# Exponentials written into the tile that will hold the state, four states ahead, and scanned in place

## The chip, the core and the metric

The kernel runs on one core of one Trainium2 chip. The metric is the device time of one execution in microseconds (us). Before the change three timed runs took 11246.39, 11232.78 and 11244.71 us; the median is 11244.71 us. The core has five engines that each work through their own list of instructions in order and wait for one another by semaphores: TensorE (PE in the profile, its weight loads PEld), VectorE (DVE), ScalarE (ACT), GpSimd (POOL), and SyncE (SP), which issues the DMAs.

## The reference, cut to what matters

The program is a two-layer block on eight images of 64x64 pixels with 96 channels. What fills the time is the selective scan of the first layer, which runs along four orders of the pixels (`K` = 4: two diagonals, each in both directions), over 192 channels with 16 states for each channel:

```python
delta = jax.nn.softplus(dts + dt_projs_bias[None, :, :, None])
A = -jnp.exp(A_logs).reshape(K, D_INNER, D_STATE)
...
def step(hst, inp):
    u_t, d_t, B_t, C_t = inp
    hst = hst * jnp.exp(d_t[..., None] * A) + (d_t * u_t)[..., None] * B_t[:, :, None, :]
    return (hst, jnp.einsum('bkdn,bkn->bkd', hst, C_t))
```

For every channel and every state n this is a first-order recurrence along the 4096 pixels: the decay `exp(delta * A_n)` multiplies the old state, the feed `delta * u * B_n` is added, and the result times `C_n` is summed over the 16 states. Around it lie a group norm, a projection, a 3x3 convolution, a layer norm and an output projection; after it come linear attention and a feed-forward layer.

## The kernel before, in words

**Steps and states.** One image is cut into 8 chunks of 512 pixels, and each chunk is scanned once forwards (q = 0) and once backwards (q = 1). That makes 8 x 2 x 8 = 128 steps. A step has 16 states (n = 0 to 15, here called places), so the main loop of `run` (line 1155) passes 2048 states, numbered i = 16m + n. A tile of one state is 128 partitions by 3 groups by 512 pixels: two diagonals with 64 channels each on the partitions, 192 = 3 x 64 channels in the groups g = 0, 1, 2.

**What one state needs.**
- `decay(i)` (line 961): three exponentials on ACT, one for each group, line 966.
- The feed, which stands in three PSUM banks, `feed[0]` to `feed[2]`, that all states share. It is made in one of three ways, by the letter of the place in `FEED = "DADADAGADADAAAAA"` (line 48). Letter A (10 places): eight copies with a scale on ACT, line 988, write the tile feedT (two buffers), and `turn(i, g)` transposes it into bank g, four transposes for each group, line 996. Letter G (place 6): the same with three products on POOL (line 979). Letter D (places 0, 2, 4, 8 and 10): ACT makes nothing; one matmul (line 998) spreads a row into `feed[0]`, and three products on DVE (line 1013) fill the three banks.
- `recur(i)` (line 1000): three scans on DVE (line 1009), one for each group; each reads its decays, its feed bank and the last column of the step before (carry), and writes the state tile h.
- `keep(i)` and `read(i)` (lines 1021 and 1027): POOL copies the last column into carry (line 1025) and multiplies h in place by the row C (line 1030; the row comes by two DMAs of `fetch`, line 952).
- `reduce(i, part)` (line 1032): PE transposes h and sums it in PSUM, twelve transposes in three parts of four, line 1044. Every part reads columns of all of h, so h is free only after part 2.

**The order.** Nothing is reordered by a scheduler: each engine executes in the order in which the loop writes the instructions. Iteration i of the loop writes
- for ACT: `decay(i+2)`, then other stages' ACT work (`work.at("A")`), then the eight copies of `times_b(i+2)`;
- for DVE: the products and scans of state i, with other stages' DVE work ahead of the third scan;
- for PE: `turn(i+1, 0)`, `reduce(i-4, 0)`, other work, `turn(i+1, 1)`, `reduce(i-4, 1)`, other work, `turn(i+1, 2)`, `reduce(i-4, 2)`, other work;
- for POOL: `keep(i-1)` and `read(i-1)`; for SP: `fetch(i+4)`.

The other work comes from `Work` (line 261), which hands out pieces of the remaining stages of the neighbouring images by a credit in microseconds for each iteration: the convolution (line 542), the walk along the diagonals (lines 587 to 596), the tail (lines 608 to 836), and `prologue` (line 879), which makes rows, delta and du of a step that is about two steps ahead. The longest pieces on ACT are softplus (line 921, with a load of a table before and after it) and SiLU (lines 558 and 559).

**Buffers around the change.** Tiles come from a pool; a tile's tag has a fixed number of buffers, used in turn, and the first instruction that writes a new tile waits until the last instruction that uses the buffer's old tile has ended. Before, decays have three buffers and h has six. So `decay(i+2)` takes the buffer of `decay(i-1)` and waits for the third scan of state i-1, and the first scan of state i takes the buffer of h(i-6). In all 3 + 6 = 9 tiles of 128 x 1536 float32.

Of the kernel before, what the change touches and what calls it, by code (L numbers as in the profile page):

```python
# [9 lines left out]
F32 = mybir.dt.float32  # L10
F16 = mybir.dt.float16
F8 = mybir.dt.float8e5
AF = mybir.ActivationFunctionType
ALU = mybir.AluOpType
# [3 lines left out]
P = 128  # L18
# [13 lines left out]
T = 512  # L32
# [3 lines left out]
G = 3  # L36
# [802 lines left out]
def run(tc, psum, dram, x, out, w, NB):  # L839
# [9 lines left out]
    nc = tc.nc  # L849
    scans = ExitStack()  # L850
    pool = scans.enter_context(tc.tile_pool(name="scan", bufs=1))
# [3 lines left out]
    total = len(steps) * NS  # L855
# [15 lines left out]
            )  # L871
        return images[b]

    made, decays, feeds, hs, carry, sums, other = {}, {}, {}, {}, {}, {}, {}
    feed = [psum.tile([P, T], F32, tag=f"feed{g}", name=f"feed{g}") for g in range(G)]
    banks = [psum.tile([P, T], F32, tag=f"bank{i}", name=f"bank{i}") for i in range(2)]
    work = Work(banks + feed)
# [62 lines left out]
    def bring(m):  # L940

        b, q, c = steps[m]
        work.finish(lambda: c in image(b).walked)
        u = pool.tile([P, G, T], F32, tag="u", name=f"u_{m}", bufs=2)
        made[m] = SimpleNamespace(u=u, c={}, multiplied=False)
        for d in range(2):
            nc.sync.dma_start(
                out=u[d * GC : (d + 1) * GC],
                in_=image(b).seq[d][:, c * T : (c + 1) * T].rearrange("(g i) t -> i g t", i=GC),
            )  # L950

    def fetch(i):

        m, n = divmod(i, NS)
        cc = made[m].c[n] = pool.tile([P, T], F32, tag="cc", name=f"cc_{i}", bufs=5)
        for d in range(2):
            nc.sync.dma_start(
                out=cc[d * GC : (d + 1) * GC], in_=made[m].crow[d * NS + n : d * NS + n + 1, :].to_broadcast([GC, T])
            )

    def decay(i):
        m, n = divmod(i, NS)
        _, q, _ = steps[m]
        decays[i] = pool.tile([P, G, T], F32, tag="decay", name=f"decay_{i}", bufs=3)
        for g in range(G):
            nc.scalar.activation(decays[i][:, g, :], made[m].delta[:, g, :], AF.Exp, scale=w.a_neg[:, q, g, n : n + 1])  # L966

    def times_b(i):

        m, n = divmod(i, NS)  # L970
        o = made[m]
        if FEED[n] == "D":
            return
        f = feeds[i] = pool.tile([P, TB * G, P], F32, tag="feedT", name=f"feedT_{i}", bufs=2)
        if FEED[n] == "G":
            d = 2
            scale = o.rows[:, :, XB : XB + d * NS].rearrange("p j (d n) -> p j d n", d=d)[:, :, :, n]
            for g in range(G):
                nc.gpsimd.tensor_tensor(  # L979
                    f.rearrange("p (j g) (d c) -> p g j d c", g=G, d=d)[:, g],  # L980
                    o.duT.rearrange("p (j g) (d c) -> p g j d c", g=G, d=d)[:, g],
                    scale.unsqueeze(3).to_broadcast([P, TB, d, GC]), ALU.mult,
                )
            return
        for j in range(TB):
            for d in range(2):
                part = (slice(None), slice(j * G, (j + 1) * G), slice(d * GC, (d + 1) * GC))
                nc.scalar.activation(  # L988
                    f[part], o.duT[part], AF.Copy, scale=o.rows[:, j, XB + d * NS + n : XB + d * NS + n + 1]
                )  # L990

    def turn(i, g):
        m, n = divmod(i, NS)
        if FEED[n] != "D":
            for j in range(TB):
                nc.tensor.transpose(feed[g][:, j * P : (j + 1) * P], feeds[i][:, j * G + g, :], w.ident)  # L996
        elif g == 0:
            nc.tensor.matmul(feed[0], w.pick[:, FEED[:n].count("D"), :], made[m].x, start=True, stop=True)  # L998

    def recur(i):  # L1000
        m, n = divmod(i, NS)
        _, q, _ = steps[m]
        h = hs[i] = pool.tile([P, G, T], F32, tag="h", name=f"h_{i}", bufs=6)
        a = decays.pop(i)
        back = slice(None, None, -1) if q else slice(None)

        def scan(g):
            init = carry[m - 1][:, n, g : g + 1] if m % NST else 0.0
            nc.vector.tensor_tensor_scan(h[:, g, back], a[:, g, back], feed[g][:, back], init, ALU.mult, ALU.add)  # L1009

        if FEED[n] == "D":
            for g in (1, 2, 0):
                nc.vector.tensor_tensor(feed[g], feed[0], made[m].du[:, g, :], ALU.mult)  # L1013
        if n == FEED.rindex("D"):
            made[m].multiplied = True
        scan(0)
        scan(1)
        work.at("V")
        scan(2)
# [12 lines left out]
    def reduce(i, part):  # L1032
        m, n = divmod(i, NS)
        b, q, c = steps[m]
        if n == 0 and part == 0:
            sums[m] = psum.tile([P, TB * G, P], F32, tag="y", name=f"y_{m}")
        if q and n == 8 and part == 0:
            other[m] = pool.tile([P, TB * 2 * DI], F32, tag="y0", name=f"y0_{m}")
            nc.sync.dma_start(out=other[m], in_=image(b).part[:, c, :])
        y = sums[m]  # L1040
        some = range(4 * part, 4 * part + 4)
        for j in some:
            r, g = divmod(j, G)
            nc.tensor.matmul(  # L1044
                y[:, j, :], hs[i][:, g, r * P : (r + 1) * P], w.ident, is_transpose=True,
                start=(n == 0 and j % 4 == 0), stop=(n == NS - 1), skip_group_check=True,
            )
        if q and n in (1, 2, 3) and part == 2:
            for j in range(4 * (n - 1), 4 * n):
                r, g = divmod(j, G)  # L1050
                nc.tensor.matmul(
                    y[:, j, :], made[m].u[:, g, r * P : (r + 1) * P], w.skip[:, g, :],
                    start=False, stop=False, skip_group_check=True,
                )
        if part == 2:
            hs.pop(i)

    def place(m):

        b, q, c = steps[m]
        y = sums.pop(m)
        ys = pool.tile([P, TB * 2 * DI], F32, tag="ys", name=f"ys_{m}")
        rows = ys.rearrange("p (d k c) -> p d k c", d=2, k=TB)
        for d in range(2):
            nc.scalar.copy(
                rows[:, d].rearrange("p k (g i) -> p k g i", i=GC),
                y.rearrange("p (k g) (d i) -> p d k g i", g=G, d=2)[:, d],
            )  # L1070
        if q == 0:
            nc.sync.dma_start(out=image(b).part[:, c, :], in_=ys)
        else:
            work.start(spread(m, rows), urgent=True)
# [20 lines left out]
    def before(b):  # L1095
        return measures(tc, work, pool, x, w, image(b), b)
# [4 lines left out]
    def between(b):  # L1101
        if b + 1 < NB:
            yield from begin(b + 1)
        if b > 0:
            yield from end(b - 1)
# [17 lines left out]
    def all_done():  # L1123
        return not (work.streams or work.jobs)
# [20 lines left out]
    LAG = 4  # L1145
    for i in range(4):
        fetch(i)
    for i in range(2):
        decay(i)
        times_b(i)  # L1150
    for g in range(G):
        turn(0, g)
# [2 lines left out]
    for i in range(total + LAG + 1):  # L1155
        m, n = divmod(i, NS)
        b, at = divmod(i, PER)
        if i < total:
            if at == LAG + 3 and b:
                work.finish(lambda: all_done() and not other)  # L1160
                work.finish(all_done)
                work.stream(between(b))
            if at == PER // 2 and b + 2 < NB:
                work.stream(before(b + 2))
            if n == NS - 3 and m + 2 < len(steps):
                work.start(prologue(m + 2), urgent=True)
            if n == NS // 2 and m + 2 < len(steps):
                bring(m + 2)
        work.next()
        if i + 2 < total:  # L1170
            decay(i + 2)
        work.at("A")
        if i + 2 < total:
            times_b(i + 2)
        if i < total:
            recur(i)
        else:
            work.at("V")
        for part in range(3):
            if i + 1 < total:  # L1180
                turn(i + 1, part)
            if 0 <= i - LAG < total:
                reduce(i - LAG, part)
            work.at("P", part)
        if 0 <= i - LAG < total and (i - LAG) % NS == NS - 1:
            place((i - LAG) // NS)
        if 0 <= i - 1 < total:
            keep(i - 1)
            read(i - 1)
        work.at("G")  # L1190
        if i + 4 < total:
            fetch(i + 4)
        feeds.pop(i, None)
# [86 lines left out]
```

## Time and profile before

| what | value |
|---|---|
| median of three timed runs | 11244.71 us |
| profiled execution, span from first to last instruction | 11243.9 us |
| mean granted TensorE clock in it | 0.907 of full speed |
| start of the first scan, end of the last scan | 244.2 us, 10996.3 us |
| scans (line 1009) | 6144, 1201 to 1262 ns each |
| exponentials (line 966) | 6144, 714 ns each |
| copies of feedT (line 988) | 10240, 445 ns each |
| transposes of feedT and of h (lines 996 and 1044) | 16896 and 24576 |
| products of h with C on POOL (line 1030) | 2048, 3457 ns each |

The page gives the span of the profiled execution; its own time as a whole is not listed apart, and the span is 0.8 us below the median of the timed runs. Of the span, 10752 us lie between the first and the last scan: 5.25 us for one state, 84.0 us for one step. The table of waits lists for each pair "engine, tile and line of who waited <- who ended the wait" the total in us, how often, and the longest. In a timeline each line has the start and the duration in us, the engine, the line of the kernel, the operation, the tile written and the tiles read, the shapes and the count of merged instructions; in square brackets stands how long the engine had been idle just before, and what ended that.

### The profile page before, as it was taken

To read this page: it belongs to the slowest core of one execution; us is meant where nothing else is said; L and a number is where in the kernel's file an instruction comes from. 1 tells how busy PE (TensorE), PEld (TensorE's weight loads), DVE (VectorE), ACT (ScalarE), POOL (GpSimd) and SP (SyncE) were. 2 spreads that over 40 slices of the span, in tenths; PEclk is the share of its full clock that TensorE was granted. 3 is DMA by queue.
4 is the path that set the end of the run, shared out by engine and by line. 5 is a ranking of instruction groups with operands and counts; after the bars stand their busy time and mean duration, and the time that the engine had idled before them with its cause. 6 is when DMAs were issued, how large, how long until landed. Compare 5 with 4: busy or idle time off the path is not lost.

```text
span 11243.9 us, 182845 instructions
## 1 busy us (share of the span) xinstructions
PE 9140.0 (81%) x60885; PEld 7661.4 (68%) x60885; DVE 9396.9 (84%) x10582; ACT 9455.9 (84%) x19651; POOL 9365.4 (83%) x7047
## 2 busy tenths in 40 slices
PE   6888788878888788878888788887888878878884
PEld 5677677666676667766677666776667666666663
DVE  2988988888888888888888888888898888989993
ACT  3888888888888888888888888888898888888883
POOL 1877987899878998789987899779997799998994
PEclk8999999888998889988999898998999988889886
DMA  3335333543335443354334543345433543432332
GB/s 91 106 92 143 100 98 92 144 118 102 97 93 149 110 108 95 96 144 113 102 92 113 138 107 102 92 118 134 109 99 90 133 119 104 108 103 84 99 94 63
DMA packets 1122742, 1206.98 MB, mean 107 GB/s; under 512 B 452790, under 2 KB 730007, under 8 KB 1121799
## 3 DMA queue, kind: packets, MB, share of 16 engines
q1 hardware_dynamic: 1121798, 1195.28, 40.3%
q8 instruction: 485, 7.95, 0.3%
q14 instruction: 459, 3.75, 0.1%
HBM read 874.83 MB, written 319.98 MB: 106 GB/s over the span
## 4 chain that ended last, share of the span: by engine, by line
PE 24%; ACT 23%; DVE 17%; POOL 14%; issue 10%; DMA 7%; SPq 4%; DVEq 0%; POOLq 0%; ACTq 0%
DVE h L1009 11%; ACT feedT L988 9%; POOL h L1030 8%; ACT decay L966 7%; PE y L1044 7%; PE feed L996 7%; DMA cc<-crow 4%; DVE feed L1013 4%; PE bank L542 3%; SPq L587 2%; PE bank L894 2%; PE feed L998 1%; ACT L63 1%; POOL du L928 1%; DMA y<-wide 1%
## 5 line engine op out<-in xcount | busy, mean ns | idle before, releaser
L1030 POOL TENSOR_TENSOR h<-h,cc 128x1536 f32<-128x1536 f32 x2048 | 7079.9, 3457 | 458.3 <-DMA cc<-crow 228.9
L1009 DVE TENSOR_TENSOR_SCAN h<-decay,carry,feed 128x512 f32<-128x512 f32 x5376 | 6514.2, 1262 | 810.2 <-PE feed L996 704.8
L966 ACT ACTIVATE decay<-delta,a_neg 128x512 f32<-128x512 f32 x6144 | 3975.0, 714 | 1116.4 <-DVE h L1009 1114.4
L996 PE MATMUL feed<-ident,feedT 128*128 128x128 f32 x16896 | 3090.8, 303 | 1649.1 <-DVE h L1009 1084.6
L1044 PE MATMUL y<-ident,h 128*128 128x128 f32 x24576 | 3847.4, 290 | 130.7 <-POOL h L1030 47.4
L996 PEld LDWEIGHTS feed<-ident,feedT 128*128 128x128 f32 x16896 | 2209.1, 155 | 2246.9 <-ACT feedT L988 840.8
L988 ACT ACTIVATE feedT<-duT,rows 128x192 f32<-128x192 f32 x10240 | 3673.7, 445 | 17.6 <-PE feed L996 14.7
L1044 PEld LDWEIGHTS y<-ident,h 128*128 128x128 f32 x24576 | 3164.5, 152 | 525.2 <-issue 410.3
L1013 DVE TENSOR_TENSOR feed<-feed,du 128x512 f32<-128x512 f32 x1920 | 1200.4, 685 | 162.2 <-PE feed L998 146.5
L1025 POOL COPY carry<-h 128x3 f32<-128x3 f32 x2048 | 402.5, 197 | 877.0 <-DVE h L1009 803.2
L1009 DVE TENSOR_TENSOR_SCAN h<-decay,feed 128x512 f32<-128x512 f32 x768 | 879.5, 1201 | 118.9 <-PE feed L996 106.8
L542 PE MATMUL bank<-wf,xp 97*128 97x192 f32 x4266 | 851.9, 332 | 0.0
L998 PE MATMUL feed<-x,pick 77*128 77x512 f32 x1280 | 708.8, 636 | 3.9
L542 PEld LDWEIGHTS bank<-wf,xp 97*128 97x128 f32 x4266 | 692.8, 194 | 5.4 <-issue 4.6
L928 POOL TENSOR_TENSOR du<-delta,u 128x1536 f32<-128x1536 f32 x128 | 448.4, 3503 | 188.8 <-ACT delta L921 188.8
L916 PE MATMUL bank<-x,ws 13*128 13x512 f32 x764 | 435.5, 650 | 5.6 <-ACT x L907 5.6
L979 POOL TENSOR_TENSOR feedT<-duT,rows 128x512 f32<-128x512 f32 x384 | 396.2, 1060 | 4.7 <-PE feed L996 4.7
L894 PE MATMUL bank<-wx,u 128*128 128x77 f32 x3048 | 360.0, 275 | 0.0
L894 PEld LDWEIGHTS bank<-wx,u 128*128 128x128 f32 x3048 | 352.3, 193 | 1.9 <-ACT duT L936 0.2
L918 DVE COPY delta<-bank 128x512 f32<-128x512 f32 x382 | 256.7, 672 | 86.5 <-PE bank L916 86.1
L934 PE MATMUL bank<-ident,du 128*128 128x128 f32 x1532 | 251.8, 291 | 65.1 <-POOL du L928 61.8
L998 PEld LDWEIGHTS feed<-x,pick 77*128 77x128 f32 x1280 | 211.5, 200 | 97.6 <-DVE h L1009 44.8
(261 smaller groups left out, 6957.4 us busy)
## 6 DMA issues: line engine op xcount, KB each, us to landing
cc<-crow SPq DMA_DIRECT2D x4096, 128.0 KB
u<-seq SPq DMA_DIRECT2D x256, 384.0 KB
wide<-ys SPq DMA_DIRECT2D x512, 192.0 KB
ut<-image SPq DMA_DIRECT2D x768, 64.0 KB
seq<-us SPq DMA_DIRECT2D x128, 384.0 KB
part<-ys SPq DMA_DIRECT2D x64, 768.0 KB
y<-part SPq DMA_DIRECT2D x64, 768.0 KB
y<-wide SPq DMA_DIRECT2D x256, 192.0 KB
```

Of the source, the lines that this page charges most:

```text
L542: nc.tensor.matmul(v[:, j, :], flat[:, o : o + P], k.wf[:, i, :], start=(i == 0), stop=(i == 8), skip_group_check=True)
L894: nc.tensor.matmul(v[:, j, :], u[:, g, j * P : (j + 1) * P], w.wx[:, q, g, :], start=(g == 0), stop=(g == G - 1))
L916: nc.tensor.matmul(ps, w.ws[:, q, g, :], x[0 : 2 * NR + 1, :], start=True, stop=True)
L928: nc.gpsimd.tensor_tensor(du, delta, u, ALU.mult)
L966: nc.scalar.activation(decays[i][:, g, :], made[m].delta[:, g, :], AF.Exp, scale=w.a_neg[:, q, g, n : n + 1])
L988: nc.scalar.activation(f[part], o.duT[part], AF.Copy, scale=o.rows[:, j, XB + d * NS + n : XB + d * NS + n + 1])
L996: nc.tensor.transpose(feed[g][:, j * P : (j + 1) * P], feeds[i][:, j * G + g, :], w.ident)
L998: nc.tensor.matmul(feed[0], w.pick[:, FEED[:n].count("D"), :], made[m].x, start=True, stop=True)
L1009: nc.vector.tensor_tensor_scan(h[:, g, back], a[:, g, back], feed[g][:, back], init, ALU.mult, ALU.add)
L1013: nc.vector.tensor_tensor(feed[g], feed[0], made[m].du[:, g, :], ALU.mult)
L1030: nc.gpsimd.tensor_tensor(hs[i], hs[i], c.unsqueeze(1).to_broadcast([P, G, T]), ALU.mult)
L1044: nc.tensor.matmul(y[:, j, :], hs[i][:, g, r * P : (r + 1) * P], w.ident, is_transpose=True, start=(n == 0 and j % 4 == 0), stop=(n == NS ...
```

## The change

The tag decay with its three buffers is gone, and h has nine buffers. `decay(i)` takes the h tile and writes the exponentials into it; the scan reads its decays from h and writes the states over them. In the loop `decay(i+4)` stands where `decay(i+2)` stood, and four states' decays are written ahead of the loop where it was two. `times_b(i+2)`, the turns, the reductions and everything else keep their places. The buffer of `decay(i+4)` is now that of state i-5.

```diff
     def decay(i):
         m, n = divmod(i, NS)
         _, q, _ = steps[m]
-        decays[i] = pool.tile([P, G, T], F32, tag="decay", name=f"decay_{i}", bufs=3)
+        h = hs[i] = pool.tile([P, G, T], F32, tag="h", name=f"h_{i}", bufs=9)
         for g in range(G):
-            nc.scalar.activation(decays[i][:, g, :], made[m].delta[:, g, :], AF.Exp, scale=w.a_neg[:, q, g, n : n + 1])
+            nc.scalar.activation(h[:, g, :], made[m].delta[:, g, :], AF.Exp, scale=w.a_neg[:, q, g, n : n + 1])
...
     def recur(i):
         m, n = divmod(i, NS)
         _, q, _ = steps[m]
-        h = hs[i] = pool.tile([P, G, T], F32, tag="h", name=f"h_{i}", bufs=6)
-        a = decays.pop(i)
+        h = hs[i]
         back = slice(None, None, -1) if q else slice(None)
...
-            nc.vector.tensor_tensor_scan(h[:, g, back], a[:, g, back], feed[g][:, back], init, ALU.mult, ALU.add)
+            nc.vector.tensor_tensor_scan(h[:, g, back], h[:, g, back], feed[g][:, back], init, ALU.mult, ALU.add)
...
     LAG = 4
     for i in range(4):
         fetch(i)
+    for i in range(4):
+        decay(i)
     for i in range(2):
-        decay(i)
         times_b(i)
...
         work.next()
-        if i + 2 < total:
-            decay(i + 2)
+        if i + 4 < total:
+            decay(i + 4)
         work.at("A")
         if i + 2 < total:
             times_b(i + 2)
```

More of the change, by code (lines that the diff above doesn't have):

```diff
@@ L872, in image @@
         return images[b]
-    made, decays, feeds, hs, carry, sums, other = {}, {}, {}, {}, {}, {}, {}
+    made, feeds, hs, carry, sums, other = {}, {}, {}, {}, {}, {}
     feed = [psum.tile([P, T], F32, tag=f"feed{g}", name=f"feed{g}") for g in range(G)]
```

## The prediction

> **What bounds the kernel now.** I read the page first: the busy shares and the chain that ended last.
>
> ```profile
> PE 9140.0 (81%) x60885; PEld 7661.4 (68%) x60885; DVE 9396.9 (84%) x10582; ACT 9455.9 (84%) x19651; POOL 9365.4 (83%) x7047
> PE 24%; ACT 23%; DVE 17%; POOL 14%; issue 10%; DMA 7%; SPq 4%; DVEq 0%; POOLq 0%; ACTq 0%
> ```
>
> Four engines are busy for 81 to 84% each, and the chain changes hands among them. No engine bounds the kernel; the handovers do. So the table of waits comes next, then the rows of what waited ahead of the scans (last line below).
>
> ```profile
> ACT decay L966 <- DVE h L1009: 1114.4, 556, 7.3
> PE feed L996 <- DVE h L1009: 1084.6, 747, 8.1
> PEld feed L996 <- ACT feedT L988: 840.8, 1010, 4.7
> DVE h L1009 <- PE feed L996: 811.6, 729, 4.4
> PE feed L996 <- ACT feedT L988: 435.1, 757, 4.5
> ...
>   ACT decay L966: 6.7, 7
> ```
>
> The largest wait is the one that the change aims at: ACT idles 1114.4 us because `decay(i+2)` must not overwrite `decay(i-1)` before it is scanned. But DVE hardly ever waits for decays: 6.7 us in 7 cases. It waits for feeds (811.6 us), and PE waits in turn for feedT, ACT's copies (435.1 us; the PEld line is largely the same stalls seen by the weight loads). ACT writes those copies after the decays of the same iteration. So the start of the decays matters only through the copies behind it.
>
> **What the new wait is.** `decay(i+4)` takes the buffer of state i-5, whose last user is part 2 of `reduce(i-5)`. PE executes that in iteration i-1, right behind part 2 of `turn(i)`, and that turn overwrites a feed bank that the third scan of state i-1 has to have read. So if state i has letter A or G, the new wait ends after the old one by the order of PE's list: four turns plus four reductions later. If i has letter D there is no third turn, and the reduction can end earlier. The timeline around state 931 (place 3) shows both events:
>
> ```profile
> 5117.50 3.59 DVE L1009 TENSOR_TENSOR_SCAN h<-decay,carry,feed 128x512 f32<-128x512 f32 x3
> 5118.81 1.11 PE L996 MATMUL feed<-ident,feedT 128*128 128x128 f32 x4 [2.52 <-DVE h L1009]
> 5118.85 1.95 ACT L966 ACTIVATE decay<-delta,a_neg 128x512 f32<-128x512 f32 x3 [3.30 <-DVE h L1009]
> 5119.71 1.06 PE L1044 MATMUL y<-ident,h 128*128 128x128 f32 x4
> 5120.81 1.28 ACT L921 ACT_TABLE_LOAD   x1
> 5122.11 1.49 ACT L921 ACTIVATE delta<-delta 128x1536 f32<-128x1536 f32 x1
> 5123.60 1.28 ACT L63 ACT_TABLE_LOAD   x1
> 5124.89 2.88 ACT L988 ACTIVATE feedT<-duT,rows 128x192 f32<-128x192 f32 x8
> 5126.85 0.60 PE L996 MATMUL feed<-ident,feedT 128*128 128x128 f32 x3 [1.22 <-DVE h L1009]
> 5127.82 0.33 PE L996 MATMUL feed<-ident,feedT 128*128 128x128 f32 x1 [0.36 <-ACT feedT L988]
> ```
>
> The first scan of the three is the third one of state 930; it ends near 5118.8. ACT, idle for 3.30 us, starts its decays at once (5118.85). PE turns group 2 of state 931 and then does part 2 of the reduction of state 926, which ends at 5119.71 + 1.06 = 5120.77. With the change ACT would start there: 1.92 us later. Behind it in ACT's list stand softplus with its two table loads and the eight copies for state 933, which end at 5127.77; PE's fourth turn starts 0.05 us after that (5127.82), so it was waiting. The 1.92 us land on the feed of state 933.
>
> **The sum.** I took the same four times from the trace for every state j = i+2: start of its decays, end of part 2 of the reduction of state j-7, end of its last copy, start of PE's fourth turn. Late = the second minus the first, if positive. Margin = the fourth minus the third, less the 0.06 us that PE takes anyway. What is left of late after margin delays the feed.
> - 1177 of 2041 starts would be late, 1690 us in all: 956 at states with letter A (1468 us), 221 at letter D (221 us), none at G. Of 562 starts where ACT now really waits for a scan, 537 would be late, by 1.11 us in the median: the old wait is replaced by a longer one.
> - Only letter A has copies behind the decays. After their margins 546 us of the 1468 are left: place 1 24, place 3 46, place 5 154, place 7 166, places 9 and 11 18, place 12 24, place 13 80, places 14 and 15 33. Places 5 and 7 weigh most, because softplus lies there in ACT's list and the copies are late already.
> - Where ACT has no idle time, a late start moves its next start too. Carrying the lateness on until an idle stretch or a counted delay takes it up, 546 becomes 669 us.
> - Of the 546 us, 418 lie where the chain of work runs over PE, ACT or DVE, and 128 where it runs mostly over POOL, SP and DMA, so that a late feed may be taken up. I count the first share, 418/546 of 669 = 512, and half of the rest, 78: 590 us.
> - PE's clock: where it was half speed at the reduction's end (110 of 1277 states with letter A), 1.26 us are left on average, elsewhere 0.35 us. PE is now idle 2087 us ahead of its matmuls; 590 more is a factor of 1.28. If the half-speed states grow by 1.4, to be careful, that is 44 states x 0.91 = 40 us.
>
> Together 590 + 40 = 630 us on the profiled span of 11243.9 us, which is 0.8 us below the median of the timed runs: about 11870 us.
>
> The row above shows four turns in 1.11 us after 2.52 us of idleness; at full clock (5126.85) three of them take 0.60 us. [...]
>
> **The small edits.**
> - Scan in place: no scan in the trace does this. Nearest rows on both sides: POOL's product in place takes 3457 ns (line 1030) against 3503 ns between different tiles of the same shape (line 928), 1.3% less; ACT in place (line 816) 722 ns against 714 ns (line 966), 1.1% more. On 1262 ns that is -16 to +14 ns a scan, -100 to +86 us of DVE; scans hold 11% of the chain, so -11 to +9 us. I take 0.
> - Semaphores: the exponentials now wait for up to three engines, and the compiled lists show 2630 extra waits on ACT, at 17 ns (ACT's own rows before line 966): 45 us. The scans drop some 1600 to 2160 waits on POOL, at 21 ns: 34 to 45 us less on DVE. They cancel; bounds -45 to +45.
> - Two more decays ahead of the loop: 3.9 us on ACT once, hidden if the first turn is late for another reason; 0 to 4, I take 0.
> - POOL, SP, PE and the DMAs keep their lists; no instruction moves past another there.
> - The longer lead itself: at most the 6.7 us that DVE waits for decays.
>
> **The rivals.**
> - *Lockstep.* The waits feed one another: PE waits for ACT's copies, ACT for PE's reduction, the clock drops, margins vanish. Price: all late starts land, 1690 us: 12930 us. For it: the loop reduction, decays, copies, turns, reduction spans two iterations and holds 1.95 + 2.88 + 6 x 0.44 = 7.5 us plus ACT's other work; two iterations are 10.5 us, so with 4.1 us of softplus inside it is over. Against it: softplus comes once in 16 states.
> - *Little lands.* Delays are made up before they reach POOL, SP or the tail. Price: only place 5, where ACT is the chain: 154 us, 11398 us. For it: 14% + 7% + 4% of the chain is POOL, DMA and SPq.
> - *Nothing changes.* The new wait ends at about the same time as the old; it holds for D states alone. 11244 us.
> - *Faster.* The old wait goes and the new one never ends last, because the reduction runs as soon as the first scan frees a bank. Then each feed gains the smaller of ACT's wait and its own lateness: 213 us in all, 152 of it in place 5: 11031 us. It decides only if part 2 of the reduction ends ahead of the third scan; in the trace that is so for 11% of the iterations with letter D and for none with A or G. [...]
>
> **Chances and range.** Forecast 0.80, lockstep 0.07, little lands 0.07, nothing changes 0.03, faster 0.03. The low end is what lands where PE's margin is zero, 243 us late in 320 states, less the 45 us of semaphores: 11440 us. The high end lies short of all 1468 us at letter A (12712), since margins are seen in the trace: 12500 us. Faster by over 0.2% (about what a measurement of this kernel can tell) 0.03, within 0.03, slower 0.94.
>
> **What would show it.** Right: "ACT decay <- DVE" shrinks to little and a row of ACT waiting at line 966 for the reduction (line 1043 after) takes its place with more than 1114 us; PE's waits for feedT and DVE's for feeds grow by several hundred us together; the granted clock falls below 0.907; scans keep 1.2 to 1.26 us. Wrong: the new row is far below 1114 us, or it is large and the waits for feedT stay (then the margins are larger than I read), or the scans' own duration moves.

## The result and the profile after

The changed kernel takes 11742.61 us in the median of four runs (11740.68 to 11752.32), against 11245.55 us before: a ratio of 1.0444, 95% interval 1.0429 to 1.0459. It is slower by 497 us. The forecast was 11870 us; its sum gave 630 us more.

The page of the changed kernel, span and busy time:

```profile
span 11738.9 us, 182427 instructions
PE 9372.9 (80%) x60885; PEld 7749.0 (66%) x60885; DVE 9411.0 (80%) x10582; ACT 9462.2 (81%) x19651; POOL 9366.8 (80%) x7047
```

ACT is busy for 9462.2 us where it was 9455.9, DVE for 9411.0 where it was 9396.9. On these two the work is the same, and nearly all of the 495 us that the span grew are idle time. PE has the same 60885 matmuls and is busy for 9372.9 us where it was 9140.0. Of these 233 us more, 186 belong to the turns at line 996 (3090.8 us before, 3276.8 after): they wait for ACT's copies one by one, as the last timeline of this section shows (0.33 us for each there, 0.60 us for four in one go), and more of them run at the lower clock: of the 16896, 2796 start at half speed before and 3078 after (see the section on the prediction). How much each of the two adds was not measured.

(The page's chain of work breaks off here after a few per cent of the span, so it is not read.) The table of waits says where:

```profile
DVE h L1008 <- PE feed L996: 1291.5, 937, 5.4
ACT h L966 <- PE y L1043: 1141.0, 487, 11.0
...
PE feed L996 <- ACT feedT L988: 861.6, 1486, 5.2
...
ACT h L966 <- issue: 406.0, 236, 5.8
...
ACT h L966 <- POOL carry L1024: 239.6, 113, 6.2
```

The row "decay L966 <- DVE h", 1114.4 us, is gone. In its place ACT waits at the same line 966 for the reduction (line 1044, now 1043). The three rows of line 966 belong together: the profile puts a wait for several semaphores down to one of them. Compared time by time, 884 of the 889 waits of over 0.1 us at line 966 end within 0.1 us of the end of part 2 of the reduction of the state that is nine before the one whose decays are waiting (i-5 for i+4), 1855 us in all. Further down, PE's wait for ACT's copies went from 435.1 to 861.6 us and DVE's wait for feeds from 811.6 to 1291.5 us, 480 us more. For decays DVE waits no longer than before (4.8 us after, 6.7 before), so the delay reaches it through the feeds.

The groups by shape show the scan, now in place, and ACT's exponentials with the idle time ahead of them, first before, then after:

```profile
L1009 DVE TENSOR_TENSOR_SCAN h<-decay,carry,feed 128x512 f32<-128x512 f32 x5376 | 6514.2, 1262 | 810.2 <-PE feed L996 704.8
L966 ACT ACTIVATE decay<-delta,a_neg 128x512 f32<-128x512 f32 x6144 | 3975.0, 714 | 1116.4 <-DVE h L1009 1114.4
```

```profile
L1008 DVE TENSOR_TENSOR_SCAN h<-h,carry,feed 128x512 f32<-128x512 f32 x5376 | 6531.2, 1263 | 1215.4 <-PE feed L996 1129.1 <-POOL carry L1024 9.9 <-POOL y L832 7.3
L966 ACT ACTIVATE h<-delta,a_neg 128x512 f32<-128x512 f32 x6144 | 3980.2, 712 | 1867.2 <-PE y L1043 1141.0 <-issue 406.0 <-POOL carry L1024 239.6
```

A scan in place takes 1263 ns, between two tiles it took 1262. ACT idles 1867.2 us ahead of line 966 where it was 1116.4.

The timeline around the decays for place 9, which ACT writes ahead of the copies for place 7, shows one of these waits:

```profile
5347.71 4.79 DVE L1008 TENSOR_TENSOR_SCAN h<-h,carry,feed 128x512 f32<-128x512 f32 x4 [3.25 <-PE feed L996]
...
5348.60 0.60 PE L1043 MATMUL y<-ident,h 128*128 128x128 f32 x4
5349.04 0.60 PE L996 MATMUL feed<-ident,feedT 128*128 128x128 f32 x4
5349.30 1.96 ACT L966 ACTIVATE h<-delta,a_neg 128x512 f32<-128x512 f32 x3 [3.03 <-PE y L1043]
...
5353.28 2.87 ACT L988 ACTIVATE feedT<-duT,rows 128x192 f32<-128x192 f32 x8
...
5355.51 0.33 PE L996 MATMUL feed<-ident,feedT 128*128 128x128 f32 x1 [0.36 <-ACT feedT L988]
...
5356.20 0.33 PE L996 MATMUL feed<-ident,feedT 128*128 128x128 f32 x1 [0.36 <-ACT feedT L988]
5356.57 2.45 DVE L1008 TENSOR_TENSOR_SCAN h<-h,carry,feed 128x512 f32<-128x512 f32 x2 [1.45 <-PE feed L996]
```

ACT stands idle for 3.03 us. PE's reduction ends at 5348.60 + 0.60 = 5349.20, and ACT starts at 5349.30. The copies, behind the decays and 2 us of other work, start at 5353.28; PE takes them one by one as they come (each turn has waited 0.36 us), and DVE stands for 1.45 us.

### The profile page after: what moved, and what is told of

Its sections match the earlier page's. It is cut to its first block, busy times and chain, and to the rows that moved or that the text cites. A ratio compares the mean times of both kernels' runs of the same rounds, so it can differ in the third digit from the quotient of the medians.

```text
span 11738.9 us, 182427 instructions
## 1 busy us (share of the span) xinstructions
PE 9372.9 (80%) x60885; PEld 7749.0 (66%) x60885; DVE 9411.0 (80%) x10582; ACT 9462.2 (81%) x19651; POOL 9366.8 (80%) x7047
## 5 line engine op out<-in xcount | busy, mean ns | idle before, releaser
L1008 DVE TENSOR_TENSOR_SCAN h<-h,carry,feed 128x512 f32<-128x512 f32 x5376 | 6531.2, 1263 | 1215.4 <-PE feed L996 1129.1
L966 ACT ACTIVATE h<-delta,a_neg 128x512 f32<-128x512 f32 x6144 | 3980.2, 712 | 1867.2 <-PE y L1043 1141.0
L996 PE MATMUL feed<-ident,feedT 128*128 128x128 f32 x16896 | 3276.8, 308 | 1969.8 <-DVE h L1008 1023.5
L996 PEld LDWEIGHTS feed<-ident,feedT 128*128 128x128 f32 x16896 | 2258.4, 156 | 2717.3 <-ACT feedT L988 1757.8
L1008 DVE TENSOR_TENSOR_SCAN h<-h,feed 128x512 f32<-128x512 f32 x768 | 882.7, 1202 | 169.8 <-PE feed L996 162.4
L542 PE MATMUL bank<-wf,xp 97*128 97x192 f32 x4266 | 884.3, 341 | 0.0
L542 PEld LDWEIGHTS bank<-wf,xp 97*128 97x128 f32 x4266 | 720.4, 201 | 5.6 <-issue 4.6
L894 PE MATMUL bank<-wx,u 128*128 128x77 f32 x3048 | 384.6, 286 | 0.0
L894 PEld LDWEIGHTS bank<-wx,u 128*128 128x128 f32 x3048 | 377.0, 204 | 2.1 <-ACT duT L936 0.2
L1079 POOL TENSOR_TENSOR ys<-ys,y 128x768 f32<-128x768 f32 x128 | 237.7, 1857 | 51.2 <-ACT ys L1066 50.9
```

The costliest lines, as they stand in the source:

```text
L542: nc.tensor.matmul(v[:, j, :], flat[:, o : o + P], k.wf[:, i, :], start=(i == 0), stop=(i == 8), skip_group_check=True)
L894: nc.tensor.matmul(v[:, j, :], u[:, g, j * P : (j + 1) * P], w.wx[:, q, g, :], start=(g == 0), stop=(g == G - 1))
L966: nc.scalar.activation(h[:, g, :], made[m].delta[:, g, :], AF.Exp, scale=w.a_neg[:, q, g, n : n + 1])
L1008: nc.vector.tensor_tensor_scan(h[:, g, back], h[:, g, back], feed[g][:, back], init, ALU.mult, ALU.add)
```

## The experiments

All times are medians of four runs or more, with the ratio to the kernel before, run on the same chip, and its 95% interval. The theory: the buffer that the decays take is released too late, and the wait costs because the copies stand behind it. The rivals: the scan in place or the extra semaphores cost the time, or the lead of four states does.

**Two ahead, nine buffers, in place.** Only the lead goes back; the buffer is then that of state i-7. Counted back from the iteration i in which ACT writes the decays, the buffer's old state has the age seven here and five in the changed kernel.

```diff
-    for i in range(4):
+    for i in range(2):
         decay(i)
...
-        if i + 4 < total:
-            decay(i + 4)
+        if i + 2 < total:
+            decay(i + 2)
```

> In place with nine buffers, but decays two states ahead. Theory (the age of the buffer): decay(i+2) now takes the buffer of state i-7, whose reduction PE ended two iterations earlier; ACT's wait at line 966, 1867 us of idleness after the change, falls below 100 us, and the time falls below 11246 us, at most by the 213 us that the waits of before were worth: 11030 to 11246 us. Rival (scanning in place or the extra semaphores cost the time): they are unchanged here, so 11600 us or more.

Measured: 11089.39 us, ratio 0.9855 (0.9838 to 0.9871): 163 us faster than the kernel before. ACT's groups in this run, with the idle time ahead of each in the last column, and then the copy of a step's sums in the kernel before:

```profile
L966 ACT ACTIVATE h<-delta,a_neg 128x512 f32<-128x512 f32 x6144 | 3950.9, 714 | 0.4
...
L1066 ACT COPY ys<-y 128x768 f32<-128x768 f32 x256 | 189.9, 792 | 214.7 <-PE y L1043 214.6
```

```profile
L1067 ACT COPY ys<-y 128x768 f32<-128x768 f32 x256 | 188.8, 787 | 17.8 <-issue 11.7 <-PE y L1044 6.0
```

ACT no longer waits at line 966 (0.4 us). The scan in place takes 1261 ns. So the scan in place did not make the change slow. This run does not settle the semaphores by itself, since it has fewer: the trace shows 644 semaphore instructions of ACT at line 966 here, 1817 after the change and 202 before. At 17 ns each (the median) the 1615 more of the change are an estimate of 27 us, against 497; DVE's at the scans fell from 3907 to 2306. With the old wait gone the kernel gains 163 us, where the working of the "faster" rival gave 213. It had put 152 of these in place 5; measured between the first scans, 36 us are gained from place 4 to 5, 204 from 5 to 6, and 73 are lost from 6 to 8, so that the sums are near and the places are not. What is new is 214.7 us of idle time ahead of the copy of a step's sums; two later runs turn on it.

**Two ahead, seven buffers.** The run before with `bufs=7` in place of `bufs=9`: the lead of the kernel before, the wait of the changed one.

> In place, decays two states ahead, and only seven buffers, so that decay(i+2) waits for the reduction of state i-5, as in the changed kernel, with the lead of the kernel before. Theory (the age of the buffer): the lead is worth nothing, the wait is the same, so 11700 to 11800 us. Rival (the four-state lead itself costs, by ACT's work done too early): near the kernel before, 11250 to 11400 us.

Measured: 11745.19 us, ratio 1.044 (1.0424 to 1.0455), as the changed kernel. ACT's row:

```profile
L966 ACT ACTIVATE h<-delta,a_neg 128x512 f32<-128x512 f32 x6144 | 3980.0, 712 | 1883.7 <-PE y L1043 1169.6 <-issue 372.5 <-POOL carry L1024 258.0
```

The idle time, 1883.7 us, is close to that of the changed kernel (1867.2). At the same age of the buffer's old state, five, two states of lead and four take the same time; against the run before, only the age differs. The rival of the lead falls.

**Copies first.** The changed kernel, four ahead and nine buffers, with the decays last in ACT's iteration.

```diff
         work.next()
-        if i + 4 < total:
-            decay(i + 4)
         work.at("A")
         if i + 2 < total:
             times_b(i + 2)
+        if i + 4 < total:
+            decay(i + 4)
```

> The changed kernel with one move: in each iteration ACT does its other work and the eight copies first and the decays for state i+4 last. The buffers and the wait are the same. Theory (the wait costs by what stands behind it): the copies no longer stand behind a wait in their own iteration, and the reduction is mostly done when ACT gets there: 11050 to 11300 us, ACT's idle time at line 966 below 500 us. Rival (the extra semaphores, the scan in place, or PE's clock): no gain, 11650 us or more.

Measured: 11127.85 us, ratio 0.989 (0.9875 to 0.9905), with 165.9 us of idle time at line 966:

```profile
L966 ACT ACTIVATE h<-delta,a_neg 128x512 f32<-128x512 f32 x6144 | 3959.9, 713 | 165.9 <-issue 92.0 <-PE y L1043 68.0 <-POOL carry L1024 3.9
```

The buffers are the same and the wait is for the same reduction, but by the time ACT has made the copies it is nearly always over. So the place of the wait in ACT's list is what costs the time, and neither the scan in place nor the number of buffers. The move takes the decays behind ACT's other work as well as behind the copies; that the copies are what is late is read from the waits for them, not from this run alone.

**Reduction three states behind.** The changed kernel with `LAG = 3`: the buffer comes free one iteration earlier.

> The changed kernel with the reduction three states behind in place of four, so that part 2 of the reduction of state i-5 is written one iteration earlier for PE and the buffer comes free about 5 us earlier. Theory (the age of the buffer): most of the 497 us come back, less what PE now waits for POOL's product, since POOL has one state less of room (PE's waits for POOL were 100 us before): 11100 to 11450 us. Rival (the lead, the semaphores or the scan in place): no gain, 11700 us or more.

Measured: 11368.38 us, ratio 1.0103 (1.0088 to 1.0118). The wait at line 966 is gone (83.2 us), and 374 of the 497 us came back. The expectation held in its size and failed in its reason. PE's matmuls and weight loads of the reduction stood idle until POOL's product for 158.9 us where it was 100.3, and 59 us more are too little for what is still missing. But ACT idled ahead of the copy of a step's sums (line 1066), 706.9 us in 128 cases, once in each step:

```profile
ACT ys L1066 <- PE y L1043: 706.9, 128, 13.0
```

Cut up by places, this run lost 272 us against the kernel before between the first scans of places 4 and 5, and gained 161 us over all others. The run with two ahead gained 160 us in all, with 204 us at place 6, where this run gained 67, so only the sums agree.

**Three ahead, nine buffers.** As the first experiment with three in place of two: the buffer of state i-6.

> In place with nine buffers, decays three states ahead: the buffer is that of state i-6, whose reduction stands one iteration earlier in PE's list than in the changed kernel, about 5 us. Late starts were 1.11 us in the median, so theory (the age of the buffer) gives almost no wait at line 966 (below 150 us, as in the run with the reduction three states behind) and a time near the run with two ahead: 11080 to 11150 us. Rival (each state of lead costs its share): halfway between 11089 and 11743 us, 11350 to 11450 us.

Measured: 11092.74 us, ratio 0.986 (0.9845 to 0.9875), the same as with two ahead; ACT idles 127 us at line 966. Between an old state of age six and one of age five lie 650 us, between six and seven nothing.

**Two ahead, nine buffers, copies first; three ahead, nine buffers, copies first.** The move of the third experiment in the first and in the fifth.

> In place, nine buffers, decays two ahead, and the copies ahead of the decays in ACT's list. Theory: neither the copies nor the decays wait for a buffer any more, and the copies come 2 us earlier in each iteration, which helps where they were late (places 5, 7 and 13 to 15); DVE may begin to wait for decays at letter D, since they now come last with two states of lead. 10950 to 11120 us. Rival (the copies' place is worth nothing once the wait is gone): 11080 to 11100 us, as with two ahead and decays first.

> As the run before with the decays three ahead. Theory: at the time when ACT reaches the decays, after the copies, the reduction of state i-6 has long ended, and DVE has a state more of lead: as fast as two ahead with the copies first or up to 50 us faster, 10930 to 11100 us. Rival (lead costs): slower than that run by 100 us or more.

Measured: 11119.22 us (0.9882, 0.9866 to 0.9899) and 11117.06 us (0.9882, 0.9867 to 0.9897). Both lie at the upper end of, or above, what the theory gave; once no wait is in the way, putting the copies first brings nothing, and both medians lie some 25 to 30 us above the runs with decays first, with intervals that overlap. By places the largest difference is one stretch: between the first scans of places 5 and 6 these two gain 94 and 96 us against the kernel before, where two and three ahead with decays first gain 204 and 195. With two ahead DVE does wait for decays, 182.2 us in 129 cases. With three ahead the time is the same, so that wait is not what makes the difference; ACT's own wait ahead of the copies, 224.3 us for the turn that frees their buffer (144.8 us with decays first), is a candidate that was not tested by itself. So is PE's clock: its granted mean is 0.906 and 0.907 in these two traces, 0.915 and 0.916 in the two with decays first.

**The kernel before, copies first.** Separate tiles, three and six buffers, and only ACT's order changed.

> The kernel before (separate tiles, three buffers for decays) with the copies ahead of the decays. Theory (a wait costs by what stands behind it): the old wait for the scan, 1114 us of idleness, no longer stands ahead of copies in its own iteration, so some of the 213 us that it was worth come back: 11050 to 11240 us. Rival (that wait cost nothing, the gain of the nine buffers has another cause): 11240 us or more.

Measured: 11144.9 us, ratio 0.9906 (0.9891 to 0.9921). ACT's wait for the scan falls from 1114.4 to 37.3 us. Moving the three exponentials of each iteration is worth 103 us in the kernel before, without a single buffer changed; 197 us of DVE waiting for decays appear with it.

**Two ahead, nine buffers, reduction three or five states behind.** The first experiment with `LAG = 3` and with `LAG = 5`. They ask what held the run with the reduction three behind, and whether the 214.7 us ahead of the sums' copy can be had.

> The fastest kernel so far (in place, nine buffers, two ahead, 11089 us) with the reduction three states behind. With the reduction three behind and four ahead it was 11368 us, with ACT idle 707 us ahead of the copy of the step's sums (line 1066), which then stands one iteration earlier in ACT's list, ahead of the copies for place 5. Theory (that copy, not the buffer, held that run): the same wait appears here though no decay waits for a buffer, 11300 to 11400 us, all of the rise in place 5. Rival (the buffer's age still held it): 11080 to 11150 us.

> The fastest kernel so far with the reduction five states behind: the copy of the step's sums stands one iteration later in ACT's list. In that kernel ACT still idled 215 us ahead of it. Decays take the buffer of state i-7, reduced in the iteration before last, so they should not wait. Theory: that idleness shrinks and part of it comes back, 10950 to 11090 us. Rival (the later copy holds up PE's first reduction of the next step, or the shorter age of the buffer brings the wait back): 11100 us or more.

Measured: 11358.32 us (1.0098, 1.0081 to 1.0115) and 11238.49 us (0.9993, 0.9983 to 1.0002). In the first no decay waits for a buffer (0.3 us at line 966), and it is as slow as with four ahead; the rise is again 272 us at place 5. The waits of the two runs for the sums' copy, three behind first:

```profile
ACT ys L1066 <- PE y L1043: 712.4, 128, 10.8
```

```profile
ACT ys L1066 <- PE y L1043: 511.6, 124, 10.6
```

With the reduction three behind, that copy stands in ACT's list just ahead of the iteration with softplus and the copies for place 5; with five behind it stands just ahead of the iteration that makes the copies for place 7, and the loss, 189 us against the kernel before, lies between the first scans of places 6 and 7. With four behind the iteration after it makes decays and other work only, since place 6 has its feed from POOL. So five behind did not bring the idle time back; it more than doubled it, and the expectation failed. In that run ACT also waits 147.0 us at line 966, the other half of the rival; three ahead, with 127 us there, lost nothing by it. Both losses look like the mistake of the change with another instruction: a wait in ACT's list ahead of copies. No run moves the copy of the sums by itself, so this is read from the places and not shown.

## Why the prediction was right

**The new wait.** The prediction said that the decays would wait for part 2 of the reduction of state i-5, and that this ends later than the old wait did. The waits at line 966 after show it (884 of 889), and two ahead with seven buffers, which has another lead and the same wait, has the same time.

**What stands behind it.** That the wait costs by what ACT has queued behind it is shown by moving only the decays behind it: 615 us lie between the changed kernel and that run. That the copies are the urgent part is seen in the waits: PE's for feedT and DVE's for feeds grow by 427 and 480 us, DVE's for decays not at all.

**The lead, the scan in place, the semaphores.** All were put at nothing. The lead is worth nothing (seven buffers with two ahead, 2.6 us apart from nine with four). The scan in place takes 1263 against 1262 ns. (Of the rows that it was estimated from, ACT's at line 816 is of float16, so it was not as near as it looked.) The semaphores were not measured by themselves; by the counts and the 17 ns above they are worth some 27 us more on ACT, and 1601 fewer at 21 ns are 34 us less on DVE, which is the cancelling that the prediction had.

**The sum.** It gave 630 us where 497 were measured, 133 too many. Its first term, what is left of the late starts after PE's margins, was 546 us. The intervals between the first scans of successive states, after minus before and summed over the steps, come to 477 us; with the rest of the 495 us in the first step and ahead of and behind the scans. By places:

| places | left after margins, predicted | measured |
|---|---|---|
| 0 to 4 | 70 us (places 1 and 3) | -21 us |
| 5 to 8 | 320 us (places 5 and 7) | 321 us |
| 9 to 11 | 18 us | -3 us |
| 12 to 15 | 137 us | 180 us |

So the stretch with places 5 and 7 paid what it was to pay, with the delays of place 7 spread over places 6 to 8. That match is in part luck, since the measured 321 us also hold what the lower clock cost and what was carried on, which the first term leaves out. Two steps were mis-sized. The first is the delay at places 1 and 3: nothing was lost there, 91 us less than the term had for places 0 to 4; what takes it up is not settled. The second is the one after it: "Carrying the lateness on until an idle stretch or a counted delay takes it up, 546 becomes 669 us". A surplus that could be carried is seen only in the last places, 43 us, and not 123. The deduction for stretches on POOL, SP and DMA (79 us) fell short of undoing that: together they left 44 us too many.

**The clock.** The term was 40 us, with 1.4 times as many half-speed states. Counted at the start of PE's turns, those with letter A went from 132 to 172, 1.3 times, most of the rise at place 5 (25 to 58), and the granted clock from 0.907 to 0.898. PE's idle time went from 2087 to 2349 us, 262 more and not 590. The stretches at half speed (a granted clock of 0.5 in the trace) add up to 2086 us before and 2386 after. What that cost is not measured apart and lies inside the 497 us; 300 us more at half speed are 150 us of lost work at the most, an estimate from these two sums. So in these two traces more idle time of PE goes with more time at half speed, 262 us with 300. That the idle time brings the half speed about is the author's reading; no run tests it by itself.

**The rivals.** "Faster" was priced at 213 us and given 0.03 because the wait does not go away in this change. With two ahead, where it does, the gain is 163 us. The same nine buffers are 653 us apart, by the state whose buffer is taken. "Lockstep" and "little lands" had 1690 and 154 us, and 497 lie between them.

## What to carry to other kernels

A buffer is not free when the operation that you think of has read it, but when the last one in program order has: after the change the third scan of state i-5 had ended at least 17.8 us before the decays that waited at line 966 began, and 884 of the 889 waits ended with the reduction. Before merging two tiles into one, write down for both the last reader and the iteration in whose list it stands, and count the distance from there. Then look at what is queued behind the instruction that will wait: on ACT, which worked through its list in order here, the price of the wait was the lateness of the urgent work behind it, and moving that work ahead (here 103 us in the kernel before, 615 in the changed one) or taking a buffer two states older (653 us) mattered more than how many buffers there were. Nine tiles in place are the better layout here with decays two or three ahead, 11089 us against 11253 for the kernel before on the same chip; with four ahead, and the decays ahead of the copies, the same nine are 497 us slower than the kernel before.

## What the runs showed that was not expected

The price sets in between two ages: with a state of age seven or six behind the buffer 11089 and 11093 us, with age five 11745 us at two ahead and 11743 at four. And the wait that takes over once the decays are free is ACT's copy of a step's sums, which no row of the kernel before named as costly (6.0 us of waiting for PE): 214.6 us in the fastest run, 712.4 and 511.6 us when the reduction stands one state nearer or farther.
